# A Strassen step inside a product: S1 T1 of two pairs of row blocks from seven quarter products, with the edge index begun eleven calls sooner and its keys in 16 bits

## The chip, the cores and the metric

One core of one Trainium2 chip runs the kernel. The metric is the device time in microseconds of one execution. TensorE (PE) does the matrix products in f32, VectorE (DVE) and ScalarE (ACT) read its results out of PSUM and add or copy them, GpSimd (POOL) issues the indirect DMAs, and SyncE (SP) issues most of the others.

## What is computed

```python
def _rgcn(x, edge_index, edge_type, weight, root, bias):   # N, D, R, E = 1250, 1024, 8, 20000
    out = x @ root + bias
    for r in range(8):
        mask = (edge_type == r)
        mean = segment_sum(x[src] * mask, dst) / maximum(segment_sum(mask, dst), 1)
        out = out + mean @ weight[r]
    return out

h = maximum(layernorm(x), 0)
u = _rgcn(h, ...)
z = concatenate([u, h], axis=1) @ w_gate + b_gate
x = x + tanh(u) * z + h * (1 - z)
```

## The kernel before

**Matrices, blocks, products.** The kernel multiplies the 1250 rows of h by ten 1024 x 1024 matrices (`mats`: eight weights, `root`, the lower half of `w_gate`), and at the end u by the upper half of `w_gate`. Matrix s is numbered from 0. The 1250 rows are ten blocks of 128; blocks i and i + 5 are taken together as one row step i = 0 to 4. `step(s, i)` calls `product`, which multiplies the 256 rows of a row step by a matrix in seven half-size products instead of eight (Strassen's scheme in Winograd's form): A11 B11, A12 B21, S1 T1, S2 T2, S3 T3, S4 B22 and A22 T4. Each of the seven is 128 rows by 512 by 512: four `matmul` calls of 512 columns, of which each shows as two PE instructions, so eight. Sums of these products are made in PSUM where possible: S2 T2 and S3 T3 are added to the bank that holds A11 B11, and S4 B22 to the bank that holds S1 T1, after ScalarE has copied the earlier state out.

**Strassen again, over a pair of row steps.** For the row steps 0 and 1, and 2 and 3, of a matrix, some of the seven products are themselves done as a 2 x 2 scheme over the two row steps: seven quarter products (128 rows by 256 by 256, two `matmul` calls, four PE instructions, line 219) in place of eight. `Second` does it for A12 B21 and `First` for A11 B11, in every matrix from 1 on; `Third` does it for S4 B22 in every matrix from 4 on. `First` has its sums in a small buffer `room` (s1, t1, s2, t2) that is made twice per pair on DVE (`sums`, then `next_sums`). Its method `early` runs at the end of the row step before the pair, `late` at the head of the pair. In `late` the quarter product x gets its last part, ScalarE copies x to both halves of the PSUM bank `to1` (line 355), and the last quarter product is added to `to1`. `Second` runs inside the row steps by the table `fill`: in row step 1 its `first` comes right after the copy of A11 B11, and its `sixth`, which adds to the bank that `first` opened, comes after S1 T1.

**The order of the work.** Each engine works through its instructions in the order in which the program writes them (`manual_schedule`). After most of the seven products `product` calls `done()`, which calls `between(j)` with j counted from 0. That runs `beside(j)` in `step` (loads of the next matrix, sums on DVE), and then `on(j)`, which advances a generator with the work that is not matrix products by one call, except at the places in a list: (0, 0), (1, 5) and (4, 4) as (row step, j), from matrix 1 on.

**What the calls advance.** Before the edges can be gathered, the kernel sorts them into a table (`index()`): first `norms()` (layernorm of the row blocks, 22 calls) side by side with `columns()` (11 calls), then `slots()`, then `order()`. `slots` goes over 157 columns of 128 edges, four at a time, in 43 rounds of two calls each. The first call of a round has `one_hots` and `as_bf16`: on ScalarE four ACTIVATEs `is_lo` (line 1055), a Relu (line 1057) and a cast (line 1102). The second call has `look` and `count` (eight small matmuls in bf16, lines 1124 and 1069), five kinds of DVE work ending with four scans of a 128 x 128 tile (`place`, line 1145), and on ScalarE two ACTIVATEs (`to_los`, lines 1116 and 1117). `order` ends with twenty DVE scans of 1280 elements (line 1205) and touches ScalarE nowhere. Matrix 0 gives 35 calls, and matrices 1, 2 and 3 give 31 each. With `slots` at call 23, its last call is call 108, in matrix 3, and the index ends in matrix 4. From matrix 5 on the edges are gathered and summed (lines 1339, 1344).

**PSUM.** It has eight banks: four in a ring `ps`, two `ps_b`, one `ps_n`, one `ps_q`. In matrices 0 to 3 S1 T1 takes one of the ring.

## Time and profile before

| | |
|---|---|
| time, median of 14 runs | 1337.53 us (1337.29 to 1338.65) |
| the profiled execution: its own time | 1337.47 us |
| its span, first to last instruction | 1335.7 us |
| mean granted TensorE clock | 0.998 |
| PE busy | 1323.8 us, 99% |
| DVE, ACT, POOL busy | 72%, 28%, 42% |
| matmuls of 128 x 512 f32 (line 406), all banks | 2304 |
| matmuls of 128 x 256 f32 (line 219) | 1344 |

The profiled execution's own time lies 1.8 us above its span, and 0.06 us under the median of the runs. A line of the timeline has the start, the length, the engine and line, the operation, the tiles, and in brackets how long the engine sat idle before it and what ended that. "x8" is eight instructions put together. A PE instruction's own length is longer than its distance to the next start, as matmuls are pipelined.

### The profile page before, as it was taken

What the parts mean: (1) busy time and instruction counts of PE and PEld (TensorE: products, weight loads), DVE (VectorE), ACT (ScalarE), POOL (GpSimd) and SP (SyncE); (2) the same over time, 40 slices, a digit from 0 to 9 for tenths busy, and PEclk for the clock granted to TensorE, in tenths of its full rate; (3) what the DMA queues carried; (4) which work ended last, traced back from release to release, by engine and by line L of the source; (5) the groups of instructions that cost most, each with busy time, mean ns of one, the idle gap of its engine ahead of it and who ended that gap; (6) DMA issues with size and microseconds to landing.
All of it is one profiled execution on the core that took longest, in us unless ns stands there. A gap on an engine that the chain in (4) does not pass through costs nothing.

```text
span 1335.7 us, 13410 instructions
## 1 busy us (share of the span) xinstructions
PE 1323.8 (99%) x4168; PEld 722.6 (54%) x4168; DVE 957.2 (72%) x1823; ACT 372.6 (28%) x794; POOL 567.4 (42%) x509
## 2 busy tenths in 40 slices
PE   9999999999999999999999999999999999999997
PEld 5444555455455545655655565565556556544443
DVE  7753755674675467448987978897778799867875
ACT  3335556465641212111121121112121112221210
POOL 0000364654647036501454546346265555625631
PEclk9999999999999999999999999999999999999999
DMA  8745475856854241143738778868788957869961
GB/s 318 269 183 173 106 124 131 207 120 107 184 148 95 87 111 56 53 146 113 254 127 319 239 259 331 291 239 272 273 273 299 344 196 243 302 257 294 347 165 59
DMA packets 104319, 270.94 MB, mean 203 GB/s; under 512 B 20100, under 2 KB 22354, under 8 KB 104112
## 3 DMA queue, kind: packets, MB, share of 16 engines
q1 hardware_dynamic: 44048, 119.85, 29.4%
q0 software_dynamic: 44064, 118.20, 27.5%
q10 hardware_dynamic: 16128, 31.98, 7.7%
q8 instruction: 33, 0.54, 0.2%
q14 instruction: 46, 0.38, 0.1%
HBM read 212.63 MB, written 75.49 MB: 216 GB/s over the span
## 4 chain that ended last, share of the span: by engine, by line
PE 85%; issue 4%; DVE 2%; POOL 2%; DMA 1%; ACT 0%; POOLq 0%; DVEq 0%; ACTq 0%
PE ps_b L406 41%; PE ps L406 17%; PE ps L219 14%; PE ps_b L219 4%; PE ps_n L406 4%; PE ps_q L219 2%; PE ps_n L219 2%; PE ps_q L406 2%; DMA h_op<-z_dram,node 1%; POOL out_dram L746 1%; POOL got L740 0%; DVE row L1733 0%; DVE h_op L1667 0%; DVE row L1734 0%; PE ps_q L1069 0%
## 5 line engine op out<-in xcount | busy, mean ns | idle before, releaser
L406 PE MATMUL ps_b<-w,h_op 128*128 128x512 f32 x1464 | 659.6, 595 | 1.0 <-ACT row L489 0.8
L406 PEld LDWEIGHTS ps_b<-w,h_op 128*128 128x128 f32 x1464 | 273.6, 190 | 308.5 <-issue 296.9
L1339 POOL DMA_INDIRECT got<-y,idx x193 | 246.0, 1275 | 291.2 <-DVE u L1344 188.9
L1344 DVE SCALAR_TENSOR_TENSOR u<-got,w_of,u 128x1024 f32<-128x1024 f32 (+1 forms) x193 | 246.7, 1281 | 33.5 <-DMA got<-y,idx 30.9
L406 PE MATMUL ps<-w,h_op 128*128 128x512 f32 (+1 forms) x592 | 264.8, 589 | 0.1
L1163 POOL DMA_INDIRECT table<-row_col,at_i x157 | 164.1, 1045 | 186.6 <-DVE at_i L1159 133.4
L406 PEld LDWEIGHTS ps<-w,h_op 128*128 128x128 f32 x592 | 111.0, 190 | 119.2 <-issue 114.6
L431 DVE TENSOR_TENSOR row<-row 128x512 f32<-128x512 f32 x44 | 30.4, 690 | 79.6 <-ACT row L430 79.6
L430 ACT COPY row<-ps_b 128x512 f32<-128x512 f32 x53 | 31.1, 586 | 194.3 <-PE ps_b L406 194.3
L406 PE MATMUL ps_n<-w,h_op 128*128 128x512 f32 x176 | 80.1, 592 | 0.0
L489 ACT COPY row<-ps_b 128x512 f32<-128x512 f32 x54 | 31.7, 586 | 163.9 <-PE ps_b L406 163.9
L219 PE MATMUL ps<-w,h_op 128*128 128x256 f32 x288 | 74.5, 381 | 0.0
L219 PE MATMUL ps<-w,w 128*128 128x256 f32 x288 | 71.1, 380 | 0.0
L529 ACT COPY row<-ps_b 128x512 f32<-128x512 f32 x40 | 23.4, 585 | 163.6 <-PE ps_b L406 143.3
L219 PEld LDWEIGHTS ps<-w,h_op 128*128 128x128 f32 x288 | 54.0, 190 | 27.1 <-issue 21.4
L219 PE MATMUL ps<-inner,inner 128*128 128x256 f32 x264 | 67.8, 379 | 0.0
L219 PEld LDWEIGHTS ps<-w,w 128*128 128x128 f32 x288 | 54.6, 190 | 21.8 <-issue 15.8
L1145 DVE SCALAR_TENSOR_TENSOR junk<-k_bc,key_col,before 128x128 f32<-128x128 int32 x157 | 55.0, 350 | 4.2
L219 PEld LDWEIGHTS ps<-inner,inner 128*128 128x128 f32 x264 | 50.2, 190 | 14.5 <-issue 8.6
L406 PEld LDWEIGHTS ps_n<-w,h_op 128*128 128x128 f32 x176 | 33.4, 190 | 39.5 <-issue 39.2
L457 ACT COPY row<-ps_b 128x512 f32<-128x512 f32 x54 | 31.7, 587 | 75.9 <-PE ps_b L406 71.3
L1055 ACT ACTIVATE is_lo<-io,less_lo 128x128 bf16<-128x128 f32 x157 | 50.1, 391 | 0.7 <-DMA xh_dram<-xt 0.7
(238 smaller groups left out, 1469.3 us busy)
## 6 DMA issues: line engine op xcount, KB each, us to landing
y<-row SPq DMA_DIRECT2D x72, 512.0 KB
w<-in_L_gnn_weight_dram ACTq DMA_DIRECT2D x21, 1024.0 KB
w<-in_L_gnn_weight_dram SPq DMA_DIRECT2D x10, 1024.0 KB
k_bc<-keys_dram SPq DMA_DIRECT2D x39, 256.0 KB
l_bc<-los_dram SPq DMA_DIRECT2D x39, 256.0 KB
w<-in_L_gnn_w_gate_dram ACTq DMA_DIRECT2D x6, 1024.0 KB
h_dram<-h_op SPq DMA_DIRECT2D x9, 512.0 KB
u<-in_L_gnn_bias_dram SPq DMA_DIRECT2D x9, 512.0 KB
```

Of the source, the lines that this page charges most:

```text
L219: nc.tensor.matmul(p, a[:, k, :], b[:, k, :], start=(fresh and k == 0), stop=(k == 1), skip_group_check=True)
L406: nc.tensor.matmul(b[:, at], aop[:, i, k, :], w.of[i][:, k, at], start=(fresh and k == 0), stop=(k == KQ - 1), skip_group_check=True)
L430: nc.scalar.copy(d, b)
L431: nc.vector.tensor_add(c22, c if lone else c22, d)
L457: nc.scalar.copy(c11, b)
L489: nc.scalar.copy(c12, b)
L529: nc.scalar.copy(c21, b)
L1055: nc.scalar.activation(is_lo[:, i, :], io, AF.Abs, bias=less_lo[:, c0 + i:c0 + i + 1])
L1145: nc.vector.scalar_tensor_tensor(junk, o["k_bc"][:, i, :], key_col[:, c:c + 1], before, op0=OP.is_equal, op1=OP.mult, accum_out=rank[:, c: ...
L1163: ins = nc.gpsimd.indirect_dma_start(out=table[:, :], out_offset=bass.IndirectOffsetOnAxis(ap=at_i[:n, c:c + 1], axis=0), in_=row_col[:n, ...
L1339: nc.gpsimd.indirect_dma_start(out=t[:n], out_offset=None, in_=y[g][:, :], in_offset=bass.IndirectOffsetOnAxis(ap=at[:n, d, k:k + 1], axis=0),
L1344: nc.vector.scalar_tensor_tensor(u[:n], t[:n], w, u[:n], op0=OP.mult, op1=OP.add)
```

## The change

The change has three parts.

1. `Fifth`, a new class, does the 2 x 2 scheme over a pair of row steps for S1 T1, in matrices 1 to 4. Its result lies in `ps_n` for the even row step and `ps_m` for the odd one, and S4 B22 is then added to it there. `begin` runs at the head of the pair, ahead of `First.late`; `second` after that; `early` after S2 T2; `late` after S3 T3. Its sums use the same `room` as those of `First`. S1 T1 is no longer computed in either row step of the pair. `First`'s `fifth_to` goes from the call j = 3 to the head of the pair. Some of `Second`'s parts are moved in row steps 2 and 3.
2. The list of calls that give nothing to the generator has (1, 1) and (3, 1) as well. There is a new call inside the S3 T3 part, `between(TICK)`, after the copy of S3 T3 and ahead of `Fifth.late`, and the call after S2 T2 is kept, in both even row steps. So matrices 1, 2 and 3 still give 31 calls. `slots` starts when `columns` ends (call 12, not 23), while `norms` still goes on; the keys are stored and read as 16-bit numbers. In matrix 4 `beside_group` waits for the place (2, 1).
3. Two banks `ps_n` and `ps_m` hold S1 T1 in turn for all products, and the ring `ps` has three banks, not four.

```diff
@@ bank() @@
-        return psum.tile([P, 512], F32, name="ps", bufs=4)
+        return psum.tile([P, 512], F32, name="ps", bufs=3)
+    def sum_bank(odd):
+        return psum.tile([P, CG, P], F32, name=("ps_n", "ps_m")[odd], bufs=1).rearrange(
+            "p c k -> p (c k)")
...
+    class Fifth:
...
+        def begin(self):
+            self.to0 = sum_bank(0)
+            self.x = bank()[:, :H]
+            Second.add(self, self.x, self.a11, self.b11, True)
+            nc.scalar.copy(self.to0[:, :H], self.x)
+        def second(self):
+            Second.add(self, self.to0[:, :H], self.a12, self.b21)
+        def early(self):
+            y = bank()[:, :H]
+            Second.add(self, y, self.s1, self.t1, True)
+            nc.scalar.copy(self.p5, y)
+            Second.add(self, self.x, self.s2, self.t2)
+            nc.vector.tensor_add(self.to0[:, H:], self.x, self.p5)
+        def late(self):
+            self.to1 = sum_bank(1)
+            Second.add(self, self.x, self.s1, self.t1)
+            nc.scalar.copy(self.to1.rearrange("p (a n) -> p a n", a=2),
+                           self.x[:, None, :].to_broadcast([P, 2, H]))
+            Second.add(self, self.to0[:, H:], self.s2, self.b22)
+            Second.add(self, self.to1[:, :H], self.a22, self.t2)
+        def fifth_to(self):
+            nc.vector.tensor_add(self.to1[:, H:], self.to1[:, H:], self.p5)
@@ product: p7 @@
             nc.scalar.copy(d, b)
+            if root and head:
+                between(TICK)
+                root.late()
+                nc.scalar.copy(c22, c)
+                root.fifth_to()
             nc.vector.tensor_add(c22, c if lone else c22, d)
@@ product: p1 @@
                 b = first.late() if head else first.to1
+            if root and head:
+                root.sums()
+                first.fifth_to()
             nc.scalar.copy(c11, b)
+            if root and head:
+                root.second()
             done()
@@ product: p5 @@
-            if c is None:
-                c = inner.hold() if inner and inner.holds else held("ps_n")
+            if root:
+                c = root.to1
+            elif c is None:
+                c = inner.hold() if inner and inner.holds else sum_bank(odd)
                 add(c, S1, True)
@@ product: order @@
+        if root and head:
+            root.begin()
+            c = root.to0
+            if inner:
+                inner.c0 = c
+            b = p1()
+        elif first and head and early is None and "first" not in fill:
...
         done()
-        filled("sixth")
+        if root and head:
+            root.early()
+            root.next_sums()
+        if not filled("sixth") and root and head:
+            done()
@@ step: fill @@
+            elif i == 2 and root and q:
+                fill = dict(seventh=lambda: (e.first(), q.second(q.c0), True),
+                            fourth=lambda: (e.sixth(), True))
+            elif i == 2 and root:
+                fill = dict(seventh=lambda: e.first(),
+                            third=lambda: e.sixth(),
+                            fourth=lambda: (e.seventh(), e.to_first(to), True))
...
-                fill = dict(first=lambda: (e.to_second(t[0]), e.fourth_to_second(t[0]), 0)[-1],
+                fill = dict(first=lambda: (root and e.fourth(), e.to_second(t[0]),
+                                           e.fourth_to_second(t[0]), 0)[-1],
@@ load_keys @@
-                    t = now.setdefault(j, {})[name] = ix.tile([P, CG, P], I32, name=name,
+                    t = now.setdefault(j, {})[name] = ix.tile([P, CG, P], I16, name=name,
@@ index @@
         def index():
-            for _ in zip_longest(norms(), columns()):
-                yield
+            yield from columns()
+            first_part.close()
             with tc.tile_pool(name="ix", bufs=2) as ix:
                 yield from slots(ix)
...
-        todo = index()
+        todo = (None for _ in zip_longest(norms(), index()))
...
-                if s > 0 and (i, j) in ((0, 0), (1, 5), (NP - 1, 4)):
+                if s > 0 and (i, j) in ((0, 0), (1, 1), (1, 5), (3, 1), (NP - 1, 4)):
                     return
@@ beside_group @@
             yield
+            while at_call != [2, 1]:
+                yield
             passes_over()
```

More of the change, by code (lines that the diff above doesn't have):

```diff
@@ L12 @@
 I32 = mybir.dt.int32
+I16 = mybir.dt.int16
 AF = mybir.ActivationFunctionType
@@ L81, in tile_rgcn_highway @@
     LATE = 4
+    TICK = 9
+    FIFTHS = 4
     IDLE = 12
@@ L110, in tile_rgcn_highway @@
     last_dram = dram.tile([N, D], F32, name="last_dram")
-    keys_dram = dram.tile([NCH * P], I32, name="keys_dram")
-    los_dram = dram.tile([NCH * P], I32, name="los_dram")
+    keys_dram = dram.tile([NCH * P], I16, name="keys_dram")
+    los_dram = dram.tile([NCH * P], I16, name="los_dram")
     y = [dram.tile([(R0[g + 1] - R0[g]) * N, D], F32, name=f"y{g}") for g in range(G)]
@@ L284, in hold @@
         def hold(self):
-            self.c0 = psum.tile([P, CG, P], F32, name="ps_n", bufs=1).rearrange("p c k -> p (c k)")
+            self.c0 = sum_bank(0)
             return self.c0
@@ L362, in fifth_to, with __init__, sums, next_sums @@
             nc.vector.tensor_add(self.to1[:, H:], self.to1[:, H:], self.p5)
+    class Fifth:
+        def __init__(self, f, i, room, p5):
+            b = f.place["t1"]
+            self.b11, self.b12, self.b21, self.b22 = [
+                b[:, k:k + 2, c:c + H] for k in (0, 2) for c in (0, H)]
+            self.a11, self.a12, self.a21, self.a22 = [
+                h_op[i + o][:, S1, k:k + 2] for o in (0, 1) for k in (0, 2)]
+            self.t1, self.t2, self.s1, self.s2 = room
+            self.p5 = p5
+        def sums(self):
+            Third.sums(self)
+        def next_sums(self):
+            Third.next_sums(self)
+        def begin(self):
[20 more added lines that the diff above has]
+            nc.vector.tensor_add(self.to1[:, H:], self.to1[:, H:], self.p5)
     def transposed(aop, part, of, n, relu=False):
@@ L391, in product @@
                 fill=None, second=None, third=None, inner=None, first=None, early=None, own=(),
-                aside=None, head=False, lone=False):
+                aside=None, head=False, lone=False, odd=0, root=None):
         c11, c12 = to[0][:, :Q], to[0][:, Q:]
@@ L416, in filled @@
                 done()
+                return True
+            return False
         def p3():
@@ L472, in p5 @@
             return c
-        if first and head and early is None and "first" not in fill:
-            c = inner.hold() if inner else bank()
+        if root and head:
[5 more added lines that the diff above has]
+        elif first and head and early is None and "first" not in fill:
+            c = inner.hold() if inner else sum_bank(odd)
             add(c, S1, True, ks=range(KQ // 2))
@@ L557, in firsts, with fifths @@
         return s > 0
-    waiting, waiting_third, waiting_first = {}, {}, {}
+    def fifths(s):
+        return 0 < s <= FIFTHS
+    waiting, waiting_third, waiting_first, waiting_fifth = {}, {}, {}, {}
     at_call = [0, 0]
@@ L580, in step @@
             waiting[i] = Second(fac[s], i), t[0]
+            if fifths(s):
+                waiting_fifth[s, i] = Fifth(fac[s], i, room, p5_room)
         def put(i, part, t):
@@ L601, in beside @@
             if two and i % 2 == 0 and j == 3:
-                waiting_first[s, i].fifth_to()
+                if not root:
+                    waiting_first[s, i].fifth_to()
                 if i == 0:
@@ L616, in beside @@
                 Second(fac[s], 2).next_left()
-            if (s, i, j) == (0, 0, 3) or (s > 0 and (i, j) == (3, int(thirds(s)))):
+            if (s, i, j) == (0, 0, 3) or (s > 0 and (i, j) == (3, int(thirds(s) or fifths(s)))):
                 new.load_first()
@@ L645, in step @@
         coming = next_first(s, i)
+        root = waiting_fifth.get((s, i - i % 2)) if two else None
         def first_sums():
@@ L698, in step @@
             elif q:
-                fill = dict(first=lambda: (q.first(t[1][:, :Q]), e.fourth(), e.to_second(t[0]),
+                fill = dict(first=lambda: (root and (e.seventh(), e.to_first(to)),
+                                           q.first(t[1][:, :Q]), e.fourth(), e.to_second(t[0]),
                                            e.fourth_to_second(t[0]), 0)[-1],
@@ L709, in step @@
                 inner=q, first=waiting_first.get((s, i - i % 2)) if two else None,
-                head=i % 2 == 0, lone=i == NP - 1,
+                head=i % 2 == 0, lone=i == NP - 1, odd=int(i % 2 or i == NP - 1), root=root,
                 early=early if coming else None, own=("ps_q",) if s > EARLY and not two else ())
@@ L811, in tile_rgcn_highway @@
         ix1 = early.enter_context(tc.tile_pool(name="ix1", bufs=1))
+        xpool = early.enter_context(tc.tile_pool(name="xpool", bufs=3))
         first_part = early.enter_context(ExitStack())
-        xpool = first_part.enter_context(tc.tile_pool(name="xpool", bufs=3))
         def load_x(i, part, t=None, pieces=1):
@@ L993, in columns @@
             nc.vector.tensor_single_scalar(lo_i, key_i, P - 1, op=OP.bitwise_and)
-            for to, of in ((keys_dram, key_i), (los_dram, lo_i)):
+            for to, of, name in ((keys_dram, key_i, "key_h"), (los_dram, lo_i, "lo_h")):
+                half = ix0.tile([P, 2, P], I16, name=name)
+                nc.vector.tensor_copy(half, of)
+                of = half
                 nc.sync.dma_start(to[:P * P].rearrange("(c p) -> c p", p=P), of[:, 0, :])
@@ L1279, in norms, with index @@
             left(h_op[4])
+        def index():
+            yield from columns()
             first_part.close()
-        def index():
-            for _ in zip_longest(norms(), columns()):
-                yield
             with tc.tile_pool(name="ix", bufs=2) as ix:
@@ L1777, in tile_rgcn_highway @@
                 product(h_op[i % 2], fac[NM - 1], t, between=beside_u,
-                        own=("ps_n", "ps_q"),
+                        own=("ps_q",), odd=i % 2,
                         last=lambda *of: finish(1, *of))
@@ L1782, in tile_rgcn_highway @@
                 product(h_op[i % 2], fac[NM - 1], t, between=beside_last, last=finish_last,
-                        own=("ps_n", "ps_q"),
+                        own=("ps_q",), odd=i % 2,
                         pieces=2, second=lambda: None,
```

## Prediction

> **What bounds the kernel now.** The page first: how much of the span has TensorE at work.

> ```profile
> span 1335.7 us, 13410 instructions
> ...
> PE 1323.8 (99%) x4168; PEld 722.6 (54%) x4168; DVE 957.2 (72%) x1823; ACT 372.6 (28%) x794; POOL 567.4 (42%) x509
> ```

> A busy PE here is a stream without gaps. Distances from start to start in the timeline are 0.429 us for a 512-column matmul (8 of them 3.43) and 0.2155 for a 256-column one (4 of them 0.86). The waits of PE itself (sum, times, longest) are next to nothing:

> ```profile
> PE ps_b L406 <- ACT row L489: 0.8, 1, 0.8
> ...
> PE ps_b L219 <- ACT ps_b L345: 0.6, 1, 0.6
> ```

> The windows of matrices 1, 2, 3 and 4 (length, then busy time of PE, PEld, DVE, ACT):

> ```profile
> 143.40:265.30 121.90, 121.90 (x457) 65.42 (x456) 75.76 (x288) 70.29 (x172) 67.08 (x64) 1.00 0.68 146
> 265.30:387.20 121.90, 121.90 (x457) 65.44 (x456) 75.99 (x288) 70.25 (x172) 67.11 (x64) 1.00 0.69 146
> 387.20:509.10 121.90, 121.90 (x368) 64.82 (x366) 72.64 (x159) 24.48 (x53) 45.11 (x42) 1.00 0.37 96
> 509.10:624.90 115.80, 115.80 (x354) 66.29 (x353) 67.05 (x137) 20.84 (x42) 38.42 (x35) 1.00 0.25 84
> ```

> PE is busy for the whole of each, so matmul work taken out is gained, and any wait put in is lost. ACT has 70 us in matrices 1 and 2, against 21 where `slots` is absent. That is little on the average, but ACT takes its work in program order, with copies on which PE waits queued behind index work. Here is row step 1 of matrix 2, PE and then ACT:

> ```profile
> 287.11 1.11 PE L219 MATMUL ps<-w,h_op 128*128 128x256 f32 x4
> 288.06 1.03 PE L219 MATMUL ps<-w,w 128*128 128x256 f32 x4
> 288.92 3.60 PE L406 MATMUL ps<-w,h_op 128*128 128x512 f32 x8
> ```

> ```profile
> 287.09 0.59 ACT L529 COPY row<-ps_b 128x512 f32<-128x512 f32 x1 [3.32 <-PE ps_b L406]
> 287.57 1.27 ACT L1055 ACTIVATE is_lo<-io,less_lo 128x128 bf16<-128x128 f32 x4
> 288.88 0.63 ACT L1057 ACTIVATE is_lo<-is_lo 128x512 bf16<-128x512 bf16 x1
> 289.42 0.24 ACT L1102 CAST s_b<-seen 128x80 bf16<-128x80 f32 x1
> 289.56 0.58 ACT L457 COPY row<-ps_b 128x512 f32<-128x512 f32 x1
> 290.04 0.72 ACT L1116 ACTIVATE to_lo<-l_bc,less_pid 128x512 bf16<-128x512 int32 x1
> 290.79 0.63 ACT L1117 ACTIVATE to_lo<-to_lo 128x512 bf16<-128x512 bf16 x1
> 291.33 0.35 ACT L225 COPY w<-ps 128x256 f32<-128x256 f32 x1
> ```

> `Second.first` starts at 287.11; its copy (L225) runs only from 291.33. `Second.sixth` adds to that bank and must follow the copy. What fills PE meanwhile is S1 T1, from 288.92 to 292.35. That is the product the change removes. Once in the kernel the cover was short already, and PE waited for a copy behind the same ACT work:

> ```profile
> 133.72 0.33 ACT L1102 CAST s_b<-seen 128x20 bf16<-128x20 f32 x2
> 133.96 0.36 ACT L345 COPY ps_b<-ps 128x256 f32<-128x256 f32 x1
> ```

> ```profile
> 134.38 1.13 PE L219 MATMUL ps_b<-w,h_op 128*128 128x256 f32 x4 [0.55 <-ACT ps_b L345]
> ```

> **What is removed from PE.** Per pair 16 matmuls of 512 columns go (16 x 0.429 = 6.86) and 28 of 256 columns come (28 x 0.2155 = 6.03): 0.83 less, and 6.6 us over eight pairs.

> [...] The rows here give 0.2155 against 0.429, nearly exactly half, and they decide.

> **The index in order of calls.** A first half of a round costs ACT 1.31 + 0.53 + 0.25 = 2.09 us, a second half 0.76 + 0.53 = 1.29 (start to start, rows above), a 512-column copy 0.48, a 256-column one 0.25. A reader on ACT starts 0.20 after PE's last issue, a 512-column copy is done 0.585 after its start, a 256-column one 0.365, and PE follows 0.06 later. `slots` starts at call 12 and has 86 calls: up to call 97, the last of matrix 2. Even calls are first halves. So matrices 1 and 2 hold slots in every call, as before, and matrix 3 holds none on ACT.

> Let t be the end of the matmuls named; the wait is when the copy is ready, less when PE is there.

> - Row step 1, `sixth` (t: A22 T4 of row step 0). ACT: 0.20, copy 0.48, both halves 3.38, copy 0.48 = 4.54, the copy of `first` ready at 4.97. PE: small matmuls 0.31, `first` 1.72 = 2.03. Wait 2.9; from the trace above 291.75 - 288.92 = 2.8. In matrices 1 and 2: 5.8.
> - `Fifth.late` after the call TICK (t: S3 T3). The copy of S3 T3 ends its turn at 0.68; then the half. Matrix 1 (calls 38, 50, first half): 0.68 + 2.09 = 2.77, copy of x ready at 3.41; PE has x and one quarter more, 1.72. Wait 1.7, twice. Matrix 2 (69, 81, second half): 1.97, ready at 2.62, PE at 2.03. Wait 0.6, twice. Together 4.6.
> - `First.late` of the second pair (t: A22 T4 of row step 1). `begin` (0.86) stands ahead of it where half of S1 T1 (1.72) stood. Matrix 1 (call 46, first half): 2.77, copy for `begin` 0.25, ready at 3.66; PE at 2.59. Wait 1.1. Matrix 2 (second half): none.
> - Row step 3 (t: A22 T4 of row step 2). `seventh`, then `fourth` on the same bank, then S2 T2 after the copy of A11 B11, with S1 T1 gone between. Matrix 1: the copy of `seventh` is ready at 2.40 (0.68 + 1.29 + 0.43), PE at 1.39: 1.0; then a first half and the copy, ready at 4.96, PE at 3.35: 1.6. Matrix 2: 2.1 and 0.8. Matrix 3, without index on ACT, only the copy's own time: 0.6. Together 6.1.
> - Matrix 0, four transposes at 65.48: a ring of three makes the fourth wait for the first one's copy out, and that now stands behind call 14, a first half (1.84 without its cast). In the trace that copy ends at 67.39 and the fourth starts at 66.79: between 0.7 without the index work and 2.5 with it. I take 2.5.

> Sum of waits 20.1. A restart costs more: the row at 134.38 lasts 1.13, not 1.03; 13 places give 1.2. `late` itself shows 0.07 in `First`; four undisturbed places 0.3. The old wait of 0.55 at 134.38 goes, as call 33 becomes a second half.

> **Hidden.** DVE gets per pair eight sums (1.89 for four, start to start) and two adds, 4.5 us, at 76 of 122 busy: before `late` needs t1, the walk leaves 0.4 to 1.2 us; if that cover is short by one second half (DVE 2.2 to 2.8), it costs up to 2.4 a pair. The index's small matmuls only move from matrix 3 to matrix 0 (11 of 31 calls): nothing. Keys in 16 bits: 80 broadcasts halve, at 44% DMA share where they now start; SP's queue has them behind stores on which PE does not wait. ACT's read of 16-bit numbers lies between 0.63 (the bf16 row) and 0.72: at most 1 us less, taken as nothing. The scans on DVE have 0.35 either way. The POOL scatters begin sooner, with nothing behind them that PE needs. Table and gather are needed from matrix 5 on, unchanged.

> **Sum.** -6.6 - 0.55 + 20.1 + 1.2 + 0.3 = +14.4, so 1337.5 (the profiled execution, as the median) becomes 1351.9.

> **Rivals.**

> - *The waits aren't there* (ends on the other side). If ACT's halves are done before PE arrives, the 6.6 is gained: 1331. This needs all waits under 6.6, a third of those worked out. Against it is the trace: the copy at 291.33 ended 0.7 before PE needed it with 3.43 us of S1 T1 still there.
> - *Half the cover remains*: one of the two halves ahead of each copy falls elsewhere, waits 10, so 1341.
> - *DVE becomes late as well*: the sums for `late` arrive behind a second half in matrices 1 and 2: up to 4 x 2.4 = 10 on top, 1361. For it: two to four DVE jobs stand in one queue around S2 T2; against: 40% of DVE is idle there.
> - *The small matmuls are not half price after a copy*, and matrix 4, with `Third` on the same `room`, waits too: 1 to 3 us, inside the range.

> **How the numbers follow.** The waits as worked 0.74 (own range 1346 to 1357: the 0.7-to-2.5 of matrix 0, the restart of 0 to 1.2, ACT's reads, DVE's short slack); half the cover 0.09; no waits 0.08; DVE late 0.09. A measurement of this kernel tells 0.2% (2.7 us) from no change. Faster 0.09, within 0.2% 0.04 (the lower edge of the half cover), slower 0.87. Leaving out the case of no waits, most of the half cover and the upper half of the DVE case: 1342 to 1358.

> **What would show it.** Right: PE waits for ACT at L225 (before `sixth`) near 2.9 each in matrices 1 and 2, at the copy in `Fifth.late`, at L236 and L457; windows of matrices 1 and 2 near 130 and 127 us, of matrix 3 near 119 less the index matmuls that left (116), of matrix 4 near 114. Wrong: PE without gaps in matrices 1 and 2 (then about 120 each), or waits named DVE or DMA there.

## The result, and the profile after

The change makes the kernel slower: 1354.85 us, median of 6 runs (1351.70 to 1358.19), against 1337.53 before. The ratio is 1.0131, with an interval of 1.0121 to 1.0141. The profiled execution took 1355.18 us with a span of 1353.3: 17.7 and 17.6 more than before, where 14.4 was predicted.

The page first.

```profile
span 1353.3 us, 13746 instructions
...
PE 1323.3 (98%) x4264; PEld 740.3 (55%) x4264; DVE 992.8 (73%) x1905; ACT 381.1 (28%) x818; POOL 574.3 (42%) x509
```

PE's busy time is where it was (1323.8 before), although matmul work was taken out. Of its waits (sum, times, longest) these are new:

```profile
PE ps L227 <- ACT w L233: 5.3, 2, 2.7
PE ps_m L227 <- ACT ps_m L411: 3.7, 4, 1.4
PE ps L227 <- ACT w L244: 3.2, 3, 1.9
PE ps_b L461 <- ACT row L522: 1.8, 2, 1.3
PE ps_m L461 <- DVE row L324: 1.8, 1, 1.8
...
PE ps_b L227 <- ACT ps_b L363: 0.9, 1, 0.9
```

Lines 233, 244, 363 and 522 were 225, 236, 355 and 457 before; line 411 is the copy in `Fifth.late`. All but one wait for ScalarE, at the four kinds of places that the prediction named. The windows of matrices 1 to 4 (each from the first matmul of a matrix to that of the next), and one short stretch inside matrix 2:

```profile
145.10:275.20 130.10, 121.52 (x479) 69.63 (x476) 84.42 (x308) 71.28 (x175) 66.19 (x60) 1.00 0.49 103
275.20:404.90 129.70, 123.86 (x468) 70.91 (x466) 80.71 (x288) 60.58 (x149) 69.01 (x64) 0.97 0.47 96
404.90:521.50 116.60, 116.14 (x355) 66.25 (x354) 76.79 (x133) 21.77 (x44) 42.47 (x34) 1.00 0.37 95
521.50:635.60 114.10, 114.10 (x378) 70.92 (x377) 68.59 (x143) 23.25 (x48) 28.31 (x27) 1.00 0.24 84
...
304.90:308.10 3.20, 3.20 (x8) 2.57 (x9) 2.54 (x9) 1.80 (x6) 2.04 (x2) 0.51 0.93 247
```

In before, the window that the prediction gives for matrix 3 ends 3.5 us inside matrix 4. From first matmul to first matmul it is this:

```profile
387.10:505.60 118.50, 118.50 (x356) 62.68 (x355) 69.30 (x156) 24.02 (x52) 44.31 (x40) 1.00 0.36 94
```

Matrix 4, where no index work stands on ScalarE's queue, has the gain: 114.1 against 115.8. Matrices 1 and 2 lose 8.2 and 7.8; matrix 3 gains 1.9, in part because index matmuls have left it for matrix 0. The short stretch is a thing of its own: in it TensorE was granted 0.51 of its clock. Here is what stands ahead of it, row step 1 of matrix 2, the place that the prediction showed of before:

```profile
300.27 1.11 PE L227 MATMUL ps<-w,h_op 128*128 128x256 f32 x4
...
301.22 1.03 PE L227 MATMUL ps<-w,w 128*128 128x256 f32 x4
...
302.73 0.58 ACT L522 COPY row<-ps_b 128x512 f32<-128x512 f32 x1
303.20 0.72 ACT L1215 ACTIVATE to_lo<-l_bc,less_pid 128x512 bf16<-128x512 int16 x1
303.96 0.63 ACT L1216 ACTIVATE to_lo<-to_lo 128x512 bf16<-128x512 bf16 x1
304.49 0.35 ACT L233 COPY w<-ps 128x256 f32<-128x256 f32 x1
304.90 3.53 PE L227 MATMUL ps<-w,w 128*128 128x256 f32 x8 [2.65 <-ACT w L233]
```

The copy at 304.49 comes 4.22 us after `first` starts, as before (291.33 - 287.11 = 4.22). Only the 3.43 us of S1 T1 that stood between are gone, and PE sits idle for 2.65 us. Then eight matmuls of 256 columns take 3.53 us. At the same place in matrix 1, after the same wait, they take 1.99:

```profile
175.60 1.99 PE L227 MATMUL ps<-w,w 128*128 128x256 f32 x8 [2.66 <-ACT w L233]
```

The difference is the half clock.

**An account.** For every two matmuls in sequence, take the distance from start to start beyond the median distance after a matmul of that shape (0.429 us for 512 columns, 0.216 for 256). These excesses add up to 15.3 us in before and 39.4 in after: 24.1 more. By the same medians the exchanged matmuls come to 6.5 less, and 24.1 - 6.5 = 17.6 is the difference of the spans. The sum must come out, as it is bookkeeping; what it shows is where the time lies.

### The profile page after: what moved, and what is told of

It is laid out like the page before. It is cut to its first block, busy times and chain, and to the rows that moved or that the text cites. A ratio compares the mean times of both kernels' runs of the same rounds, so it can differ in the third digit from the quotient of the medians.

```text
span 1353.3 us, 13746 instructions
## 1 busy us (share of the span) xinstructions
PE 1323.3 (98%) x4264; PEld 740.3 (55%) x4264; DVE 992.8 (73%) x1905; ACT 381.1 (28%) x818; POOL 574.3 (42%) x509
## 4 chain that ended last, share of the span: by engine, by line
PE 79%; issue 7%; DMA 4%; DVE 3%; ACT 3%; POOL 3%; POOLq 0%; DVEq 0%; ACTq 0%
PE ps_b L461 38%; PE ps L227 13%; PE ps_m L461 9%; PE ps_n L461 5%; PE ps_b L227 3%; DMA got<-y,idx 3%; PE ps_n L227 2%; PE ps L461 2%; PE ps_q L227 2%; PE ps_q L461 1%; PE ps_m L227 1%; POOL got L1437 1%; DMA h_op<-z_dram,node 1%; ACT is_lo L1154 1%; PE ps L426 1%
## 5 line engine op out<-in xcount | busy, mean ns | idle before, releaser
L1262 POOL DMA_INDIRECT table<-row_col,at_i x157 | 173.2, 1103 | 170.6 <-DVE at_i L1258 105.2
L461 PE MATMUL ps_m<-w,h_op 128*128 128x512 f32 x352 | 158.9, 594 | 1.8 <-DVE row L324 1.8
L461 PEld LDWEIGHTS ps_m<-w,h_op 128*128 128x128 f32 x352 | 66.2, 190 | 78.3 <-issue 72.7
L461 PE MATMUL ps_n<-w,h_op 128*128 128x512 f32 x208 | 94.6, 593 | 0.0
L227 PE MATMUL ps<-inner,inner 128*128 128x256 f32 x360 | 91.5, 380 | 0.2 <-DVE inner L282 0.2
L227 PE MATMUL ps<-w,h_op 128*128 128x256 f32 x320 | 83.3, 383 | 3.2 <-ACT w L244 3.2
L227 PEld LDWEIGHTS ps<-inner,inner 128*128 128x128 f32 x360 | 67.9, 190 | 18.9 <-issue 9.7
L227 PEld LDWEIGHTS ps<-w,h_op 128*128 128x128 f32 x320 | 59.7, 190 | 30.4 <-issue 19.3
L461 PEld LDWEIGHTS ps_n<-w,h_op 128*128 128x128 f32 x208 | 39.2, 190 | 44.1 <-issue 43.0
L1244 DVE SCALAR_TENSOR_TENSOR junk<-k_bc,key_col,before 128x128 f32<-128x128 int16 x157 | 55.0, 350 | 4.2
```

What stands on the lines that cost most here:

```text
L227: nc.tensor.matmul(p, a[:, k, :], b[:, k, :], start=(fresh and k == 0), stop=(k == 1), skip_group_check=True)
L461: nc.tensor.matmul(b[:, at], aop[:, i, k, :], w.of[i][:, k, at], start=(fresh and k == 0), stop=(k == KQ - 1), skip_group_check=True)
L1244: nc.vector.scalar_tensor_tensor(junk, o["k_bc"][:, i, :], key_col[:, c:c + 1], before, op0=OP.is_equal, op1=OP.mult, accum_out=rank[:, c: ...
L1262: ins = nc.gpsimd.indirect_dma_start(out=table[:, :], out_offset=bass.IndirectOffsetOnAxis(ap=at_i[:n, c:c + 1], axis=0), in_=row_col[:n, ...
```

## The experiments

The theory: the change takes 6.6 us off PE, and loses it because ScalarE's copies, queued behind halves of the index, no longer have S1 T1 to cover them. Its rivals: the loss is in the earlier index, in the three-bank ring, or in the quarter products themselves.

The first four runs were on a chip on which the kernel before took 1387.76 us, 50 more than on the others; in the first of them ScalarE and VectorE stand idle for up to 12.5 us at a time in matrices 1 to 3, and the profile puts that down to something remote. The profiles taken on other chips show no such idle time of over 2 us there. What causes it stays open. Differences of a few us are hard to read on that chip, so two of the four kernels were run again elsewhere, and a third with an addition; the kernel without any quarter products was not.

### No quarter products, and quarter products in matrices 3 and 4 alone

```diff
 def fifths(s):
-    return 0 < s <= FIFTHS
+    return False                 # e2, e7: return 2 < s <= FIFTHS
...
-    if s > 0 and (i, j) in ((0, 0), (1, 1), (1, 5), (3, 1), (NP - 1, 4)):
+    if s > 0 and (i, j) in ((0, 0), (1, 5), (NP - 1, 4)) + (((1, 1), (3, 1)) if fifths(s) else ()):
```

> Only the early index, the 16-bit keys and the new bank layout are left; Fifth runs in no matrix and the two extra places in the list of skipped calls are dropped, so matrices 1 to 3 give 31 calls as before. Theory (the time went into PE waiting for ScalarE copies behind index work, because Fifth took the cover away): near the kernel before, 1337 to 1340 us, PE gaps in matrices 1 and 2 near zero, no stretch at half clock. Rival (the early index or the ring of three banks costs the time): 1345 to 1355.

> Fifth only in matrices 3 and 4, where the index leaves ScalarE alone; matrices 1 and 2 as before. Theory: 4 pairs x 0.83 = 3.3 us gained, 0.6 lost in row step 3 of matrix 3, 0.3 in late: 1334 to 1337. Rival (Fifth costs by itself, in PSUM traffic or narrow matmuls, half of the loss in each pair of matrices): 1343 to 1347.

> The kernel of e2 once more, beside the changed one. Theory: 1334 to 1337 where the kernel before takes 1338, PE gaps in matrices 1 and 2 near zero. Rival (Fifth costs by itself): 1343 to 1347.

On the slow chip: 1392.94 without any (ratio 1.0044, 1.0015 to 1.0072) and 1392.88 with matrices 3 and 4 (1.0041, 1.0013 to 1.0069), both 5 us above the kernel before, and neither as expected. As the profile of the first has waits of PE of up to 8.9 us that no kernel has on the other chips, this was not read further. Elsewhere, matrices 3 and 4 alone took 1336.81 (0.9987, 0.9977 to 0.9996), while the changed kernel on the same chip took 1355.33. No PE wait for ScalarE of over 0.65 us is left in matrices 1 to 3. This kernel keeps the earlier index, the 16-bit keys and the three banks. Of the 3.3 us that its four pairs take off, 1.2 arrive, so those three cost about 2 us at most, and what loses the rest is the quarter products beside the index's halves.

### The changed kernel again, and its waits filled

> The changed kernel itself, beside the next three on one chip. The chip of e1 to e4 ran the kernel before at 1388 us, with DVE and ACT idle for 5 to 12 us at a time in matrices 1 to 3, put down to 'remote'. Where the kernel before takes 1338 again: 1352 to 1358; on a chip like that of e1: 1400 to 1406. Both theories expect the same; it is the reference for the others.

It took 1355.33 (1.0128, 1.0110 to 1.0145). Its waits in matrices 1 to 3 are those of the first run to 0.1 us; only one stretch at half clock shows, not two.

In the next kernel PE multiplies the identity by itself while it waits in row steps 1 and 3 of matrices 1 and 2. This is work whose output is not used.

```diff
+def keep_busy(n):
+    if s in (1, 2):
+        p = bank()
+        for _ in range(n):
+            nc.tensor.matmul(p[:, :P], ident, ident, start=True, stop=True)
...
-fill = dict(first=lambda: (e.first(), q and q.first(t[1][:, :Q]), 0)[-1],
+fill = dict(first=lambda: (e.first(), keep_busy(11), q and q.first(t[1][:, :Q]), 0)[-1],
...
-fill = dict(first=lambda: (root and e.fourth(), e.to_second(t[0]), ...
+fill = dict(first=lambda: (keep_busy((0, 3, 7, 0)[min(s, 3)]), root and e.fourth(),
+                           keep_busy((0, 6, 2, 0)[min(s, 3)]), e.to_second(t[0]), ...
```

> As the changed kernel, with matmuls of no use (128 columns, into a free bank) put into PE's waits in row steps 1 and 3 of matrices 1 and 2, so that PE waits for nothing but the rest. The waits themselves stay. Theory (after a wait of 2 to 3 us the granted clock can fall to a half for 3.4 us, twice in the changed kernel's trace): no stretch at half clock outside the tail, clock 0.998, 1.5 to 4 us faster than the changed kernel and a narrower spread: 1350 to 1353 where the kernel before takes 1338. Rival (the half clock has nothing to do with the waits): same time and spread as the changed kernel, or slower by the matmuls added.

It took 1351.40 (1.0100, 1.0082 to 1.0118). PE's timeline at the place shown above:

```profile
302.33 2.62 PE L735 MATMUL ps<-ident 128*128 128x128 f32 x22
305.15 1.99 PE L227 MATMUL ps<-w,w 128*128 128x256 f32 x8 [0.20 <-ACT w L233]
```

The same eight matmuls start 4.63 us after `first` (300.52), as in after, but take 1.99, not 3.53. No stretch at half clock is left ahead of the last matmuls, in any part of the profile, and all four runs were granted 0.999 of the clock, where the four of the kernel above have 0.993 to 0.997. So here the half clock came from PE's own waits. The times alone would not show it: of the 4.4 us between the two profiled executions the stretch is 1.8, and 2.5 is the wait of matrix 8 for line 324, which was 2.75 there and is 0.25 here. The narrower spread did not come: 1350.26 to 1352.98, against 1354.27 to 1356.63.

### The call TICK behind `late`

```diff
 if root and head:
-    between(TICK)
     root.late()
     nc.scalar.copy(c22, c)
     root.fifth_to()
+    between(TICK)
```

> As the changed kernel, but the call TICK stands behind the ScalarE copies of Fifth.late and not ahead of them. Theory: the four waits in Fifth.late (1.58, 1.58, 0.58, 0.58 in the changed kernel's trace) go, the others stay: 4.3 less, 1349 to 1352. Rival (the wait only moves to the next copy): within 1 us of the changed kernel.

> The kernel of e3 (the call TICK behind the ScalarE copies of Fifth.late) on a chip where the kernel before takes 1338. Theory: the four waits in Fifth.late go (1.58, 1.58, 0.58, 0.58 in the changed kernel), the others stay: 1349 to 1352, against 1355 for the changed kernel. Rival (the wait only moves to the next copy): 1354 to 1356.

On the slow chip it took 1399.73 (1.0072, 1.0037 to 1.0107), where the changed kernel was not run, so that this can't be compared; elsewhere 1351.52 (1.0094, 1.0071 to 1.0116), as the theory had it. The waits for line 411 are gone (4.3 us); all others in matrices 1 to 3 stand. The runs spread over 6 us, from 1347.55 to 1353.66, and the profiled one has four stretches at half clock.

### The index eleven calls later

```diff
 def index():
-    yield from columns()
+    for _ in zip_longest(norms(), columns()):
+        yield
...
-todo = (None for _ in zip_longest(norms(), index()))
+todo = index()
```

> The changed kernel with the index begun at call 23 again (after all of norms); slots then run into matrix 3, with first halves at odd calls. Theory, by the same walk of the queues: waits of 7.0 us in matrix 1, 10.0 in matrix 2 and 4.1 in matrix 3 instead of 10.0, 7.0 and 0.6, so 3.5 more than the changed kernel, 0.5 less in matrix 0: 1356 to 1361. Rival (the early start is a cost, through more work in matrix 0): 2 us or more faster than the changed kernel.

It took 1353.76 (1.0120, 1.0103 to 1.0137), below the 1356 to 1361 that were expected, and no slower than the changed kernel. Eleven is an odd number, so first and second halves trade places, and with them the waits: 6.8 us in matrix 1 and 9.6 in matrix 2, where after has 9.6 and 6.8. The miss is in matrix 3, with 1.6 where 4.1 was expected. Its row step 1 meets only the last round, of one column, not four:

```profile
428.76 0.41 ACT L1215 ACTIVATE to_lo<-l_bc,less_pid 128x128 bf16<-128x128 int16 x1
...
429.42 0.35 ACT L233 COPY w<-ps 128x256 f32<-128x256 f32 x1
```

The copy comes 1.85 us after `first` (427.57), not 4.22, and PE waits 0.44. When the index begins moves the loss from matrix to matrix, but is not its cause.

### The calls moved off the places that need a copy

Now the same calls are given at other places in matrices 1 to 3: none where a copy for PE follows soon.

```diff
 # on top of TICK behind late:
-if s > 0 and (i, j) in ((0, 0), (1, 1), (1, 5), (3, 1), (NP - 1, 4)):
+if s > 0 and (i, j) in (((0, 0), (0, 5), (1, 0), (1, 5), (1, 6), (2, 5), (2, 6), (NP - 1, 4))
+                        if s < 4 else ((0, 0), (1, 1), (1, 5), (3, 1), (NP - 1, 4))):
 # e6 and e11 as well: S1 T1 of row step 4 in the ring, in late matrices
-c = inner.hold() if inner and inner.holds else sum_bank(odd)
+c = inner.hold() if inner and inner.holds else bank() if odd == 2 else sum_bank(odd)
...
-odd=int(i % 2 or i == NP - 1)
+odd=(2 if s > EARLY else 1) if i == NP - 1 else i % 2        # e11: s > R0[1], which is 5
```

> As e3, and in matrices 1 to 3 the index calls at (0,5), (1,0), (1,6), (2,5) and (2,6), which stand ahead of the copies that PE waits for, are skipped, with (1,1), (3,0) and (3,1) let through; the index ends in matrix 4. Fifth runs in matrices 1 to 4. Theory: the waits fall to about 0.4 in row step 3 of matrices 1 and 2 and 0.6 in matrix 3, no half clock, the 6.6 us of matmuls are gained: 1332 to 1336. Rival (Fifth costs by itself, or ScalarE has too much to do in matrices 1 and 2 whatever the order): 1345 to 1355.

> As e4, and S1 T1 of row step 4 takes a bank of the ring from matrix 4 on, so that it no longer waits for the DVE adds that read ps_m of row step 3 (1.75 us in matrix 8 of the changed kernel's trace). Theory: Fifth's 6.6 us are gained and the waits are some 1.8 us: 1331 to 1335 where the kernel before takes 1338, and no PE wait on ps_m. Rival (Fifth costs by itself): as the changed kernel, 1350 to 1355.

> As e6, but row step 4 takes a bank of the ring from matrix 6 on, not from matrix 4 on: in e6 matrix 5 had a PE wait of 4.25 us, as its fourth quarter product lacked a bank of the ring while a small reduction sat in DVE's queue, and half clock after it. Theory: that wait and the half clock go, 6 us less than e6: 1333 to 1337. Rival (the wait comes from the index ending in matrix 4): as e6, 1341 to 1343.

The first, on the slow chip: 1386.31 (0.9970, 0.9945 to 0.9995), the only one of those four below the kernel before. It was not run elsewhere. The second took 1341.91 (1.0027, 1.0016 to 1.0037), a miss. Its waits for ScalarE in matrices 1 to 3 were at most 0.63 us, but it brought a new one in matrix 5, with a stretch at half clock behind it:

```profile
723.30 0.27 PE L1536 MATMUL ps<-ident,most 128*1 128x128 f32 x1
...
724.80 2.28 DVE L184 TENSOR_TENSOR w<-w,w 128x2048 f32<-128x2048 f32 x1
...
728.52 0.80 PE L227 MATMUL ps<-inner,inner 128*128 128x256 f32 x1 [4.09 <-DVE beyond L1537]
```

A single small matmul took a bank of the ring, and DVE had jobs ahead of the one that reads it. With S1 T1 of row step 4 in the ring as well, three banks were one too few. The third kernel does the same from matrix 6 on, and that wait is gone. It took 1334.72 (0.9977, 0.9968 to 0.9987; 1334.64 to 1335.01 in ten runs), 2.7 us below the kernel before. Its longest waits, but for one of 1.4 at the start that before has as well:

```profile
PE ps L426 <- DVE h_op L431: 1.5, 2, 1.1
...
PE ps L227 <- ACT w L244: 1.0, 3, 0.5
```

With the same matmuls as the changed kernel, the excess is 19.2 us instead of 39.4. Against 15.3 in before that is 3.9 more; less 6.5, the 2.6 by which its span is shorter. The waits for ScalarE in matrices 1 to 3 are down from 16.9 to 1.4. So the order of the calls had eaten the gain, and 2.7 of the 6.6 us arrive. The bank of row step 4 was changed along with the order; by the other profiles it is worth the wait of matrix 8, 0.25 to 2.75 us.

### Quarter products in matrices 1 to 8

```diff
 # on top of the kernel above
-FIFTHS = 4
+FIFTHS = 8
...
-            between(j)
+            if not (s > 4 and i == 2 and j == TICK):
+                between(j)
```

> As e11, and Fifth in matrices 5 to 8 too, where the edges are gathered (the call TICK in row step 2 is dropped there, so that the gather keeps its calls). Theory: eight pairs more save 6.6 us of matmuls; DVE, at 98 of 116 us in matrix 5, gets 9 us more per matrix and its queue holds 1.28 us adds that wait for gathers, so some sums come late: 1329 to 1339. Rival (DVE becomes the bound): 1345 or more, with PE waits named DVE inner in matrices 5 to 8.

It took 1341.96 (1.0030, 1.0018 to 1.0043), between the two expectations: 7 us slower than with matrices 1 to 4, where 6.6 less was to be had. Now the waits are for DVE:

```profile
PE ps L227 <- DVE w L223: 6.1, 5, 1.6
PE ps L227 <- DVE row L255: 3.9, 2, 2.1
PE ps L227 <- DVE inner L282: 1.9, 1, 1.9
```

They lie in matrices 5 to 8, seven places of 1.4 to 2.2 us, 12.3 together, where DVE also adds up the gathered edges (1.3 us each). 12.3 - 6.6 = 5.7, and the spans differ by 6.0. DVE is busy 77% of this span; the waits come from short jobs queued behind long ones, as on ScalarE. At the second of the seven places (PE waits 1.7 us, until 761.31) the sum of line 223 stands behind two gathered adds and three other sums; these are the first and the last of that queue:

```profile
756.78 2.61 DVE L1445 SCALAR_TENSOR_TENSOR u<-got,w_of,u 128x1024 f32<-128x1024 f32 x2
...
760.84 0.42 DVE L223 TENSOR_TENSOR w<-h_op,w 128x256 f32<-128x256 f32 x1
```

## Why the prediction was right, and where not

| term | predicted | measured in after |
|---|---|---|
| matmuls, 8 pairs | -6.6 | -6.5 (counted, by the medians) |
| row step 1, `sixth`, matrices 1 and 2 | 5.8 | 2.82 + 2.82 = 5.6 |
| `Fifth.late` after TICK | 4.6 | 2 x 1.58 + 2 x 0.58 = 4.3 |
| `First.late`, second pair of matrix 1 | 1.1 | 1.1 |
| row step 3, matrices 1, 2, 3 | 6.1 | 2.5 + 2.8 + 0.6 = 5.9 |
| matrix 0, fourth transposes | 2.5 | 0.5 |
| the old wait at 134.38 | -0.55 | -0.1 |
| restarts and `late` itself | 1.5 | 1.1 (what is left over) |
| half clock, two stretches | none | 3.0 |
| matrix 8, row step 4 | none | 1.9 |
| start of the kernel | none | 0.8 |
| sum | 14.4 | 17.6 |

- **The waits in matrices 1 to 3** were the likeliest case and are there, place by place: 17.6 predicted, 16.9 measured. They could be worked out because ScalarE's order and the length of each of its jobs stood in the trace of before. The run with the index later showed the working by halves once more, with the matrices swapped. The rows give 1.99 us for a first half (287.57 to 289.56), not 2.09; that is near the 0.1 by which most of the waits behind first halves came out short. The 116 for matrix 3 does not follow from its window of 121.9, which ends too late; from 118.5 the terms lead there, and 116.6 was measured.
- **The price of narrow matmuls** was read off the rows of before, 0.2155 us for 256 columns against 0.429 for 512. In after they follow each other at 0.216 us, 0.429 for 512 columns, and matrix 4, with two pairs and no wait of over 0.15 us, is 1.7 us shorter, where 1.66 was worked out. So the rows held, and the rival of a matrix 4 that waits is out.
- **Matrix 0** was mis-sized. The step "a ring of three makes the fourth wait for the first one's copy out" failed: the fourth got a bank that DVE, not ScalarE, had emptied, so nothing of the index stood ahead of it. In the run with the index later it did wait for ScalarE's copy, without index work, for 0.65: the lower of the two figures.

```profile
66.38 0.69 DVE L431 COPY h_op<-ps 128x512 f32<-128x512 f32 x1 [1.63 <-PE ps L426]
67.12 0.66 PE L426 MATMUL ps<-ident,h_op 128*128 128x128 f32 x4 [0.35 <-DVE h_op L431]
```

- **The old wait** stayed: 0.63 of excess for 0.72 before. That call did become a second half, but the call ahead of it became a first one, so both still stand ahead of the copy, in the other order.
- **Half clock**: that a wait could cost more than its length was priced at "a restart", 1.2 us, and the restarts are there, 0.10 us behind each wait. Two stretches of 3.41 us at half clock cost 3.0 more. This is the largest term left out, and why matrix 2 took 129.7, not 127; matrix 1, with no such stretch, took 130.1 where 130 was predicted.
- **Matrix 8**: the banks `ps_n` and `ps_m` were not followed past matrix 4. Row step 4 puts S1 T1 into `ps_m`, which row step 3's addition on DVE (line 324) must have read first. It varies: 1.9 and 2.75 in the two profiles of the changed kernel, 0.25 to 0.75 in four other kernels with the same banks.
- **Hidden, as said**: the 16-bit keys (ScalarE 0.72 us as with 32 bits, the scans 0.35), and DVE, which is nowhere late in matrices 1 to 3. The rival of late DVE was right about the mechanism and wrong about the place: it decides from matrix 5 on, in the last experiment.

That the sum came within 3 us is in part luck: half clock, matrix 8 and the start, 5.7 us together, had no term, and 2.0 too much for matrix 0 hid part of that.

What stays open: why the first chip is slower, and the 0.8 us at the start of the kernel, which lay between 0 and 1 in the runs.

## What to carry to other kernels

Work that is taken off the bounding engine may have been cover for another engine's queue: before taking it out, list what the following copy stands behind, job by job, and move those jobs in the same change. Where a resource gets a new role (a bank, a ring one shorter), follow it through every stage that uses it and not only the one being changed. And in these runs some waits of TensorE of over 2 us cost more than their own length: 1.3 to 1.8 us more in the cases below.

## What the runs showed of the hardware

| idle time in one 3.41 us window | windows | followed by half clock |
|---|---|---|
| 2.15 us or more | 7 | 7 |
| 2.0 to 2.14 | 4 | 2 |
| less than 2.0 | all others | 0 |

The border is not sharp. In the four profiles of the slower chip, where stretches of up to four windows occur, all 20 such windows with 2.15 us or more are followed by half clock, and one with 1.98 is as well.

So in after the same wait of 2.82 us cost next to nothing more where it fell across two windows (matrix 1: 2.14 and 0.68 us; the eight matmuls behind it take 1.99), and 1.5 us more where most of it fell into one (matrix 2: 2.55; they take 3.53). A stretch cost 1.3 to 1.8 us in these profiles. The runs of the changed kernel go with it: the fastest (1351.70) was granted 0.997 of the clock, the slowest (1358.19) 0.992. It is not the only reason why runs of one kernel differ: the four with the waits filled, all at 0.999, still lie 2.7 us apart.
